# Layer 0's first block rearranged: x on two DMA queues, other loads issued later, tables loaded ahead, and PReLU's two signs computed on ScalarE

## The chip, the cores and the metric

The kernel runs on one core of a Trainium2 chip. The core has a matrix engine (TensorE, "PE" in the profile, with weight loads as "PEld"), a vector engine (VectorE, "DVE"), a scalar engine that computes activations from loaded tables (ScalarE, "ACT"), a general engine (GpSimd, "POOL") and SyncE ("SP"), which here only issues DMAs. Each engine takes its instructions in its own fixed order, and engines wait for each other through semaphores. ScalarE can issue DMAs too; these stand in its order between its computations.

The metric is device time in microseconds (us) of one execution. Before the change it is 2460.86 us, the median of 4 runs from 2460.74 to 2461.31.

## What is computed

The input is x of 4 images, 128 channels and 64 x 64 pixels, in float32. Layer 0 normalises x by groups of channels, makes two 64-channel projections and one of 128 channels by 1x1 convolutions with a PReLU each, and attends over all 4096 pixels. Layer 1 (a gated attention by running sums, and a routed feed-forward net) follows and is not touched.

```python
def _prelu(x, a):
    return jnp.where(x >= 0, x, a * x)
def _conv1x1(x, w, b, a):
    y = jnp.einsum('oc,nchw->nohw', w, x) + b[None, :, None, None]
    return _prelu(y, a)
...
e1 = _conv1x1(x, w1, b1, a1).reshape(N, -1, HW)
e2 = _conv1x1(x, w2, b2, a2).reshape(N, -1, HW)
asm = _conv1x1(x, wa, ba, aa).reshape(N, C, HW)
score = jax.nn.softmax(jnp.einsum('nci,ncj->nij', e1, e2), axis=2)
out = jnp.einsum('nij,ncj->nci', score, asm)
...
x = x + _L0_conv_ref(_gn(x), ...)          # layer 0
t = _to_tokens(x)
t = t + _L1_attn_ref(_ln_t(t), ...)        # layer 1
t = t + _L1_ffn_ref(_ln_t(t), ...)
```

PReLU can be written in several ways: max(y, 0) + a min(y, 0), which the kernel used, and relu(y) + (-a) relu(-y), which it uses after the change.

## The kernel before

**Tiling.** An image ("batch" b, 0 to 3) is 128 channels by 4096 pixels. It is cut into 8 blocks of 512 pixels (`NBLK`). A block k goes through these steps, each named by the tile that it makes:

- `stat(k)` (L371): VectorE's statistics of x over the block; `chain0` to `chain2` (L374 to L390) aggregate them, average them over channel groups with two small matmuls `pg`, and take a root on ScalarE, `std` (L389). That root is the only use of the sqrt table in this stretch; the exponentials use another table.
- `normal(k)` (L397): VectorE makes the normalised block `xn`.
- `project(k)`: TensorE multiplies by both projections' weights in two halves of the rows, `pe` (L416). ScalarE copies the first half out with the bias, `y` (L418); VectorE adds the second, also `y` (L419), here called the add; `prelu` makes `z` (L404) and `ee` (L407) on VectorE. Then four DMAs spread `ee` over the partitions: two copies for the queries, `e1` (L426), and two for the keys, `e2` (L429). This is the spread.
- `value(k)`: TensorE makes `pa` (L438), VectorE adds bias and second half in `ya` (L442, L445; the second is called yb in the text), then `prelu` makes `za` (L404) and `am` (L407).

`pe`, `pa` and the small matmuls share one PSUM buffer, so the projection of a block waits until yb of the block before has been computed, and `pa` waits for the add.

**Attention.** For each batch and each block `qb` of queries there are 16 steps p, each over two groups of 128 keys. `probs` multiplies keys and queries, `sc` (L471, two PSUM buffers), and ScalarE takes the exponential, `pr` (L475, three buffers); VectorE accumulates it, `acc` (L478, the first one a copy at L484). `weigh` multiplies values and `pr`, `av` (L496). On TensorE the scores of step p+1 come ahead of the weighing of step p. Step p needs keys and values of block p // 2. One step of scores and weighing takes TensorE 2.58 us. `finish` (L530 on), nine steps into the next query block, transposes the result and adds it to the residual `t`.

**Order.** All loops are unrolled, and a list scheduler fixes the order of each engine's instructions when the kernel is built. `tc.issue_after(i)` keeps what is written under it behind instruction i in that order. For batch 0, blocks 0 and 1 are prepared ahead of step 0, and blocks 2 to 7 at the even steps p = 0, 2, ..., 10 of the first query block (`own`, `work_off`). The blocks of batch b+1 are prepared during batch b, one piece (a projection or a value) at p = 2, 6 and 10.

**Loads.** The four loads of x of a batch (L327) and all loads of `t` (L521) and of layer 1's weights (`load_layer1`, L111 to L126) go through SP's queue, those of the small weights (L335) through ScalarE's. Before the change the scheduler put loads without a dependency early: loads of `t` and the layer-1 weights stand between x and the spreads of the first blocks. There are eight completion counters for DMAs, given out in turn over both queues; a DMA is issued only when the last one with its counter has landed.

The change touches `load_x`, `prelu`, `project`, `value`, and the places in the main loop that call `load_x`, `residual` and `load_layer1`.

Of the kernel before, what the change touches and what calls it, by code (L numbers as in the profile page):

```python
# [8 lines left out]
F32 = mybir.dt.float32  # L9
AF = mybir.ActivationFunctionType  # L10
# [8 lines left out]
def conv_attn_hybrid_kernel(  # L19
# [90 lines left out]
    def load_layer1(upper):  # L110
        nc.sync.dma_start(out=wks, in_=wkt.rearrange("d (h e) -> d h e", h=NH))  # L111
        nc.sync.dma_start(out=wvs, in_=wvt)

        qs = resid.tile([C, NH], F32, tag="qs", name="qs")
        nc.sync.dma_start(out=qs, in_=qt)
        nc.gpsimd.memset(qz, 0.0)
        for h in range(NH):
            nc.gpsimd.tensor_copy(qz[:, h, h // 4 : h // 4 + 1], qs[:, h : h + 1])

        for u in range(2):  # L120
            rows_u = slice(u * P // 2, (u + 1) * P // 2)
            nc.gpsimd.tensor_copy(mask[rows_u], upper[rows_u, rows_u])
        for z in range(2):
            nc.sync.dma_start(out=gws[:, z, :], in_=gwt)
            nc.sync.dma_start(out=gbs[z * E : (z + 1) * E, :], in_=gb)
        nc.sync.dma_start(out=fb1s, in_=fb1)  # L126
# [184 lines left out]
    with ExitStack() as l0:  # L311
# [8 lines left out]
        ps_av = pool("l0av", space=PSUM)  # L320
        qs_p = pool("l0q", NBLK + 1)

        def load_x(b):
            xs = one.tile([P, N], F32, tag="x", name=f"x_{b}")
            for q in range(4):
                cols = bass.ts(q, N // 4)
                nc.sync.dma_start(out=xs[:, cols], in_=x[b, :, cols])  # L327
            return xs

        xs_of = {0: load_x(0)}  # L330

        def load(name, shape, *parts):
            s = wp.tile(list(shape), F32, tag=name, name=name)
# [14 lines left out]
        aas = load("aas", [P, 1], (every[:1], aa.to_broadcast([P, 1])))  # L348
        bas = load("bas", [P, C], (every, ba.to_broadcast([P, C])))


        gavg = wp.tile([P, P], F32, tag="gavg", name="gavg")
        make_block_diagonal(nc, gavg, C // 32)
        nc.vector.tensor_scalar_mul(gavg, gavg, 32.0 / C)

        queries, keys_of, values_of = {}, {}, {}

        def preparation(b):

            xs = xs_of[b]  # L360
            stats = small.tile([P, NBLK, 6], F32, tag="stats", name=f"stats_{b}")
            mv = small.tile([P, 2], F32, tag="mv", name=f"mv_{b}")
            gst = small.tile([P, 4], F32, tag="gst", name=f"gst_{b}")
            std = small.tile([P, 2], F32, tag="std", name=f"std_{b}")

            e2 = big.tile([P, NCH // 2, P], F32, tag="e2", name=f"e2_{b}")
            am = big.tile([P, NCH, C], F32, tag="am", name=f"am_{b}")
            keys_of[b], values_of[b] = e2, am

            def stat(k):  # L370
                nc.vector.bn_stats(stats[:, k, :], xs[:, bass.ts(k, BLK)])  # L371

            def chain0():
                nc.vector.bn_aggr(mv, stats)  # L374

            def chain1():
                pg = ps_x.tile([P, 2, BLK], F32, tag="x", name=f"pg_{b}")
                nc.tensor.matmul(pg[:, 0, 0:1], gavg, mv[:, 0:1], start=True, stop=True)
                nc.vector.tensor_copy(gst[:, 0:1], pg[:, 0, 0:1])
                nc.vector.tensor_sub(gst[:, 1:2], mv[:, 0:1], gst[:, 0:1])  # L380
                nc.vector.scalar_tensor_tensor(
                    out=gst[:, 2:3], in0=gst[:, 1:2], scalar=gst[:, 1:2], in1=mv[:, 1:2],
                    op0=ALU.mult, op1=ALU.add,
                )

            def chain2():
                pg = ps_x.tile([P, 2, BLK], F32, tag="x", name=f"pg2_{b}")
                nc.tensor.matmul(pg[:, 0, 0:1], gavg, gst[:, 2:3], start=True, stop=True)
                i = nc.scalar.activation(std[:, 0:1], pg[:, 0, 0:1], AF.Sqrt, bias=eps5)  # L389
                nc.vector.reciprocal(std[:, 1:2], std[:, 0:1])  # L390
                return i.ins

            xn_of = {}

            def normal(k):
                xn = tmp.tile([P, BLK], F32, tag="xn", name=f"xn_{b}_{k}")
                nc.vector.tensor_scalar(  # L397
                    out=xn, in0=xs[:, bass.ts(k, BLK)], scalar1=gst[:, 0:1],
                    scalar2=std[:, 1:2], op0=ALU.subtract, op1=ALU.mult,
                )  # L400
                xn_of[k] = xn

            def prelu(dst, y, z, a):
                nc.vector.tensor_scalar(  # L404
                    out=z, in0=y, scalar1=0.0, scalar2=a, op0=ALU.min, op1=ALU.mult
                )
                nc.vector.scalar_tensor_tensor(  # L407
                    out=dst, in0=y, scalar=0.0, in1=z, op0=ALU.max, op1=ALU.add
                )

            def project(k):

                xn = xn_of[k]
                pe = ps_x.tile([P, 2, BLK], F32, tag="x", name=f"pe_{b}_{k}")
                for u, h in enumerate(halves):
                    nc.tensor.matmul(pe[:, u, :], w12[h, :], xn[h, :], start=True, stop=True)  # L416
                y = tmp.tile([P, BLK], F32, tag="y", name=f"y_{b}_{k}")
                nc.scalar.activation(y, pe[:, 0, :], AF.Identity, bias=b12)  # L418
                nc.vector.tensor_add(y, y, pe[:, 1, :])  # L419
                z = tmp.tile([P, BLK], F32, tag="z", name=f"z_{b}_{k}", bufs=1)  # L420
                ee = tmp.tile([P, BLK], F32, tag="ee", name=f"ee_{b}_{k}")
                prelu(ee, y, z, a12)
                e1 = qs_p.tile([P, BLK], F32, tag="e1", name=f"e1_{b}_{k}")
                queries[b, k] = e1
                for h in halves:
                    nc.sync.dma_start(out=e1[h, :], in_=ee[halves[0], :])  # L426
                by = ee.rearrange("r (j u p) -> r j u p", u=2, p=P)
                for u, h in enumerate(halves):
                    nc.sync.dma_start(  # L429
                        out=e2[h, bass.ts(k, CPB // 2), :], in_=by[halves[1], :, u, :]  # L430
                    )

            def value(k):
                xn = xn_of[k]
                pa = ps_x.tile([P, 2, CPB, C], F32, tag="x", name=f"pa_{b}_{k}")
                for c in range(CPB):
                    for u, h in enumerate(halves):
                        nc.tensor.matmul(  # L438
                            pa[:, u, c, :], xn[h, bass.ts(c, P)], was[h, :], start=True, stop=True
                        )  # L440
                y = tmp.tile([P, CPB, C], F32, tag="y", name=f"ya_{b}_{k}")
                nc.vector.tensor_tensor(  # L442
                    y, pa[:, 0], bas.unsqueeze(1).to_broadcast([P, CPB, C]), ALU.add
                )
                nc.vector.tensor_add(y, y, pa[:, 1])  # L445
                z = tmp.tile([P, CPB, C], F32, tag="z", name=f"za_{b}_{k}", bufs=1)
                prelu(am[:, bass.ts(k, CPB), :], y, z, aas)

            first = [lambda k=k: stat(k) for k in range(NBLK)] + [chain0]
            chain = [chain1, chain2]  # L450
            blocks = []
            for k in range(NBLK):
                blocks.append((lambda k=k: normal(k), lambda k=k: project(k)))
                blocks.append((lambda: None, lambda k=k: value(k)))
            return first, chain, blocks
# [62 lines left out]
        def residual(b, qb):  # L518

            at = b * NCH + qb * CPB  # L520
            nc.sync.dma_start(  # L521
                out=t[:, bass.ds(at, CPB), :],
                in_=xtok[bass.ds(at * P, CPB * P), :].rearrange("(c p) d -> p c d", p=P),
            )
# [33 lines left out]

        first, chain, blocks = preparation(0)
        for f in first + chain:  # L560
            f()
        own = blocks
        work_off(own, 4)
        nxt = probs(*steps[0])
# [2 lines left out]
        for n, (b, qb, p) in enumerate(steps):  # L567
            pr = nxt
            if own and p % 2 == 0:
                work_off(own, 2)  # L570
                if not own:
                    xs_of[1] = load_x(1)
            if n + 1 < len(steps):
                nxt = probs(*steps[n + 1])
            weigh(b, qb, p, pr)
# [4 lines left out]
            if b + 1 < B:  # L580
# [4 lines left out]
                    last_root = chain.pop(0)()  # L585
                if qb == q0 and p == 15:
                    blocks[0][0]()
            if p == 1:
                residual(b, qb)
            if p == 9 and done:  # L590
                finish(*done)
            if p in (11, 12) and done:
# [8 lines left out]
            if (b, qb, p) == (0, 1, 0):  # L601
                upper = wp.tile([P, P], F32, tag="upper", name="upper")
                make_upper_triangular(nc, upper)
                load_layer1(upper)
            if qb > q0 and p in (2, 6, 10) and b + 1 < B and blocks:
                blocks.pop(0)[1]()
                if blocks:
                    blocks[0][0]()
                elif b + 2 < B:
                    xs_of[b + 2] = load_x(b + 2)  # L610
            if p == NPR - 1:
                copied, fold = collect(b, qb)
                if n + 1 < len(steps):
# [691 lines left out]
```

## Time and profile before

| What | us |
|---|---|
| median of 4 runs | 2460.86 |
| the profiled execution: its time | 2460.14 |
| the profiled execution: its span | 2458.4 |
| TensorE busy (share of span) | 2376.6 (97%) |
| VectorE busy | 1520.0 (62%) |
| ScalarE busy | 1150.8 (47%) |
| TensorE's share of the chain that ended last | 94% |
| the exponentials, L475: 512 of 128x1024, mean | 1.024 |
| the accumulating adds, L478: 480 of 128x1024, mean | 1.222 |
| prelu on VectorE, L404: 64 of 128x512, mean | 0.486 |
| prelu on VectorE, L407: 64 of 128x512, mean | 0.693 |
| layer 1's first projection (L703) starts at | 1466.68 |

The span runs from the first to the last instruction that the profiler saw; the time has a little around it. "Busy" of TensorE is modelled: a busy TensorE is not one at its peak, but where it has no gap, no other engine holds it. A share of the whole span says little here, since the stages differ: layer 0's start, the long run of attention steps, and layer 1 have to be read one by one. The mean granted clock is 0.989.

### The profile page before, as it was taken

The page shows a single profiled execution, that of the slowest core. Times are in us where ns is not written, and L with a number is a line of the kernel's source. Part 1 is how long each engine was busy: PE and PEld are TensorE (multiplying, and loading weights), DVE is VectorE, ACT ScalarE, POOL GpSimd, SP SyncE. Part 2 cuts the span into 40 slices and gives each one's busy share as a digit, 9 for nine tenths or more (in the row PEclk, how much of TensorE's full clock was granted, in tenths as well). Part 3 has the DMA queues.
Part 4 walks back from the last instruction along what each step waited for, and adds up shares of the span by engine and source line. Part 5 has one row for each costly group of instructions (what it writes and reads, how often), then busy time and mean ns, then how long its engine had stood idle before and what let it go on. Part 6 is the DMA issues. An engine that isn't in the chain of part 4 may idle for free.

```text
span 2458.4 us, 46253 instructions
## 1 busy us (share of the span) xinstructions
PE 2376.6 (97%) x19732; PEld 1610.8 (66%) x19732; DVE 1520.0 (62%) x2680; ACT 1150.8 (47%) x1495; POOL 307.0 (12%) x370
## 2 busy tenths in 40 slices
PE   5999999999999999999999998999999999999797
PEld 3678777787777777776877764555555556555543
DVE  6766666666656666655555555666666766756524
ACT  2344343443343433434434335666666666665341
POOL 0000000000000000000000002333333333334000
PEclk9999999999999999999999999999999999999898
DMA  8100010000100000000000001212111111121495
GB/s 226 55 13 14 14 48 1 13 7 16 48 5 1 14 14 9 14 5 1 1 1 1 1 1 36 53 37 52 38 45 45 44 46 37 37 53 37 164 357 203
DMA packets 60583, 111.07 MB, mean 45 GB/s; under 512 B 10193, under 2 KB 35409, under 8 KB 60241
## 3 DMA queue, kind: packets, MB, share of 16 engines
q1 hardware_dynamic: 59072, 107.77, 14.9%
q8 instruction: 156, 2.56, 0.4%
q10 hardware_dynamic: 1296, 0.26, 0.1%
q14 instruction: 59, 0.48, 0.1%
HBM read 86.38 MB, written 8.91 MB: 39 GB/s over the span
## 4 chain that ended last, share of the span: by engine, by line
PE 94%; DVE 3%; ACT 1%; DMA 1%; issue 0%; SPq 0%; ACTq 0%; DVEq 0%
PE av L496 35%; PE sc L471 18%; PE pk L703 9%; PE pv L821 9%; PE po L857 4%; PE pt L837 2%; PE ps L722 2%; PE ph L1149 1%; PE otr L535 1%; PE po L864 1%; PE pa L438 1%; PE pl L912 1%; PE pe L416 1%; PE pp L988 1%; PE po L1176 1%; PE otr L1190 1%
## 5 line engine op out<-in xcount | busy, mean ns | idle before, releaser
L496 PE MATMUL av<-pr,am 64*128 64x512 f32 x4096 | 1092.3, 590 | 0.0
L475 ACT ACTIVATE pr<-sc 128x1024 f32<-128x1024 f32 x512 | 524.4, 1024 | 787.5 <-PE sc L471 718.7
L478 DVE TENSOR_TENSOR acc<-acc,pr 128x1024 f32<-128x1024 f32 x480 | 586.6, 1222 | 413.4 <-ACT pr L475 413.3
L496 PEld LDWEIGHTS av<-pr,am 64*128 64x128 f32 x4096 | 668.2, 187 | 233.5 <-issue 25.4
L471 PE MATMUL sc<-e,e 64*128 64x512 f32 x2048 | 652.0, 593 | 2.4 <-DMA e<-ee 2.4
L471 PEld LDWEIGHTS sc<-e,e 64*128 64x128 f32 x2048 | 336.8, 188 | 102.4 <-issue 16.7
L703 PE MATMUL pk<-xt,wks 128*128 128x512 f32 x512 | 244.2, 617 | 6.4 <-DVE inside L637 4.2
L821 PE MATMUL pv<-wvs,xt 128*128 128x512 f32 x512 | 226.8, 596 | 2.1 <-ACT v L825 2.1
L825 ACT ACTIVATE v<-pv 128x512 f32<-128x512 f32 x256 | 152.7, 597 | 69.7 <-PE pv L821 69.6
L705 ACT ACTIVATE ks<-pk 128x512 f32<-128x512 f32 x256 | 148.7, 597 | 63.0 <-PE pk L703 62.7
L821 PEld LDWEIGHTS pv<-wvs,xt 128*128 128x128 f32 x512 | 97.1, 191 | 121.1 <-issue 115.8
L809 DVE TENSOR_TENSOR em<-em,rb 128x1024 f32<-128x1024 f32 x64 | 79.5, 1244 | 156.6 <-DMA rb<-rd 149.7
L703 PEld LDWEIGHTS pk<-xt,wks 128*128 128x128 f32 x512 | 92.3, 193 | 114.3 <-issue 81.7
L857 PEld LDWEIGHTS po<-v,em 64*64 64x64 f32 x4096 | 111.4, 133 | 26.7 <-DVE before L847 26.7
L711 POOL MEMSET ew<- 128x1024 f32 x1 | 1.0, 952 | 1022.9 <-PE pa L438 1022.9
L800 POOL TENSOR_TENSOR em<-et,mask 128x1024 f32<-128x1024 f32 x64 | 120.4, 1902 | 9.2 <-ACT et L787 9.2
L96 POOL TENSOR_SCALAR xg<-t,gmv,grs 128x128 f32<-128x128 f32 x120 | 95.1, 805 | 194.9 <-DVE grs L92 139.6
L857 PE MATMUL po<-v,em 64*64 64x128 f32 x4096 | 119.2, 271 | 0.0
L759 DVE RECIPROCAL rr<-rr 128x512 f32<-128x512 f32 x32 | 107.3, 3353 | 1.1
L744 ACT ACT_TABLE_LOAD x24 | 30.8, 1283 | 119.0 <-DVE ss L743 119.0
L745 POOL COPY state<-mm 128x1 f32<-128x1 f32 x32 | 20.7, 646 | 509.2 <-DVE mm L739 509.0
L847 DVE TENSOR_TENSOR before<-before,pt 128x128 f32<-128x128 f32 x256 | 72.7, 284 | 9.7 <-PE pt L837 3.8
(160 smaller groups left out, 2122.5 us busy)
## 6 DMA issues: line engine op xcount, KB each, us to landing
rb<-rd SPq DMA_DIRECT2D x128, 256.0 KB
fw<-in_fw_dram SPq DMA_DIRECT2D x64, 512.0 KB
x<-in_x_dram SPq DMA_DIRECT2D x16, 512.0 KB
t<-in_xtok_dram SPq DMA_DIRECT2D x32, 256.0 KB
e<-ee SPq DMA_DIRECT2D x64, 128.0 KB
out_dram<-t SPq DMA_DIRECT2D x16, 512.0 KB
e<-ee SPq DMA_DIRECT2D x64, 64.0 KB
rd<-rr SPq DMA_DIRECT2D x64, 8.0 KB
```

The costliest lines, as they stand in the source:

```text
L96: i = engine.tensor_scalar(out=dst, in0=t[:, chunk, :], scalar1=mean, scalar2=rs, op0=ALU.subtract, op1=ALU.mult)
L471: nc.tensor.matmul(sc[:, u, :], e2[halves[u], p, :], e1[halves[u], :], start=True, stop=True)
L475: nc.scalar.activation(pr, sc, AF.Exp)
L478: added.append(nc.vector.tensor_add(acc, acc, pr).ins)
L496: nc.tensor.matmul(av, am[h, j, :], pr[h, u, :], start=(j == 0), stop=(j == NCH - 1))
L703: nc.tensor.matmul(pk, wks[:, h, :], xt, start=True, stop=True)
L705: nc.scalar.activation(ks, pk, AF.Silu)
L759: inverse = nc.vector.reciprocal(rr, rr).ins
L800: nc.gpsimd.tensor_tensor(em, eq.unsqueeze(2).to_broadcast([P, 2 * NH, H2]), mask.unsqueeze(1).to_broadcast([P, 2 * NH, H2]), ALU.mult,)
L821: nc.tensor.matmul(pv.rearrange("p h d -> p (h d)"), xt[:, bass.ts(2 * q + s, P)], wvs[:, bass.ts(m, BLK)], start=True, stop=True,)
L825: last = nc.scalar.activation(v[:, bass.ts(m, HPB), :], pv, AF.Silu).ins
L857: nc.tensor.matmul(po[s * H2 : (s + 1) * H2, u, q, :], aas[q][half, s, h, :], vs[2 * q + s][half, h, :], start=(q == 0 and h == 0), stop=F ...
```

## The change

The four quarters of batch 0's x go alternately through SP's and ScalarE's queue; later batches use SP's alone. The two negated slopes are computed once (`neg`). A first activation with a sqrt loads that table while x is loading, and one with an exponential, put behind the root, loads the other table. In `prelu`, z becomes relu(-y) and y becomes relu(y), both on ScalarE, except z of block 0 of batch 0, which VectorE makes; one VectorE operation joins them. `z` gets two buffers instead of one. The spread of block 0 of batch 0 goes half through each queue, and its four DMAs are issued half by half. Loads of batch 1's x, of `t` and of layer 1 are kept behind the latest spread, and `t` of a query block is loaded from step 5 on instead of step 1.

```diff
-        def load_x(b):
+        def load_x(b, queues):
             xs = one.tile([P, N], F32, tag="x", name=f"x_{b}")
             for q in range(4):
                 cols = bass.ts(q, N // 4)
-                nc.sync.dma_start(out=xs[:, cols], in_=x[b, :, cols])
+                queues[q % len(queues)].dma_start(out=xs[:, cols], in_=x[b, :, cols])
             return xs
-        xs_of = {0: load_x(0)}
+        xs_of = {0: load_x(0, (nc.sync, nc.scalar))}
...
+        neg = wp.tile([P, 2], F32, tag="neg", name="neg")
+        nc.vector.tensor_scalar_mul(neg[:, 0:1], a12, -1.0)
+        nc.vector.tensor_scalar_mul(neg[:, 1:2], aas, -1.0)
+        seed = wp.tile([P, 2], F32, tag="seed", name="seed")
+        nc.scalar.activation(seed[:, 0:1], eps5, AF.Sqrt)
...
-            def prelu(dst, y, z, a):
-                nc.vector.tensor_scalar(
-                    out=z, in0=y, scalar1=0.0, scalar2=a, op0=ALU.min, op1=ALU.mult
-                )
+            def prelu(dst, y, z, minus_a, negative):
+                if negative is nc.vector:
+                    nc.vector.tensor_scalar(
+                        out=z, in0=y, scalar1=-1.0, scalar2=0.0, op0=ALU.mult, op1=ALU.max
+                    )
+                else:
+                    nc.scalar.activation(z, y, AF.Relu, scale=-1.0)
+                nc.scalar.activation(y, y, AF.Relu)
                 nc.vector.scalar_tensor_tensor(
-                    out=dst, in0=y, scalar=0.0, in1=z, op0=ALU.max, op1=ALU.add
+                    out=dst, in0=z, scalar=minus_a, in1=y, op0=ALU.mult, op1=ALU.add
                 )
...
-                z = tmp.tile([P, BLK], F32, tag="z", name=f"z_{b}_{k}", bufs=1)
+                z = tmp.tile([P, BLK], F32, tag="z", name=f"z_{b}_{k}")
-                prelu(ee, y, z, a12)
+                prelu(ee, y, z, neg[:, 0:1], nc.vector if (b, k) == (0, 0) else nc.scalar)
-                for h in halves:
-                    nc.sync.dma_start(out=e1[h, :], in_=ee[halves[0], :])
+                queues = (nc.sync, nc.scalar) if (b, k) == (0, 0) else (nc.sync, nc.sync)
                 by = ee.rearrange("r (j u p) -> r j u p", u=2, p=P)
-                for u, h in enumerate(halves):
-                    nc.sync.dma_start(
+                for u, (h, queue) in enumerate(zip(halves, queues)):
+                    queue.dma_start(out=e1[h, :], in_=ee[halves[0], :])
+                    moved = queue.dma_start(
                         out=e2[h, bass.ts(k, CPB // 2), :], in_=by[halves[1], :, u, :]
                     )
+                if (b, k) != (0, 0):
+                    sent.append(moved.ins)
...
-                prelu(am[:, bass.ts(k, CPB), :], y, z, aas)
+                prelu(am[:, bass.ts(k, CPB), :], y, z, neg[:, 1:2], nc.scalar)
...
         for f in first + chain:
-            f()
+            root = f()
+        with tc.issue_after(root):
+            nc.scalar.activation(seed[:, 1:2], eps5, AF.Exp)
...
                 if not own:
-                    xs_of[1] = load_x(1)
+                    with tc.issue_after(sent[-1]):
+                        xs_of[1] = load_x(1, (nc.sync,))
...
-            if p == 1:
-                residual(b, qb)
+            if p == 5:
+                with tc.issue_after(sent[-1]):
+                    residual(b, qb)
...
-                load_layer1(upper)
+                with tc.issue_after(sent[-1]):
+                    load_layer1(upper)
```

More of the change, by code (lines that the diff above doesn't have):

```diff
@@ L354, in conv_attn_hybrid_kernel @@
         nc.vector.tensor_scalar_mul(gavg, gavg, 32.0 / C)
-        queries, keys_of, values_of = {}, {}, {}
+        queries, keys_of, values_of, sent = {}, {}, {}, []
         def preparation(b):
@@ L445, in value @@
                 nc.vector.tensor_add(y, y, pa[:, 1])
-                z = tmp.tile([P, CPB, C], F32, tag="z", name=f"za_{b}_{k}", bufs=1)
-                prelu(am[:, bass.ts(k, CPB), :], y, z, aas)
+                z = tmp.tile([P, CPB, C], F32, tag="z", name=f"za_{b}_{k}")
+                prelu(am[:, bass.ts(k, CPB), :], y, z, neg[:, 1:2], nc.scalar)
             first = [lambda k=k: stat(k) for k in range(NBLK)] + [chain0]
@@ L609, in conv_attn_hybrid_kernel @@
                 elif b + 2 < B:
-                    xs_of[b + 2] = load_x(b + 2)
+                    xs_of[b + 2] = load_x(b + 2, (nc.sync,))
             if p == NPR - 1:
```

## The prediction

> **What bounds the kernel now.** I read the whole-run table first (TensorE busy 97% of 2458.4 us, the chain that ended last 94% TensorE), then busy time by stretch, to see where TensorE is not full. Columns: stretch, its length, busy us and counts of TensorE, weight loads, VectorE, ScalarE, GpSimd, then granted clock, DMA share, GB/s.
>
> ```profile
> 0.00:10.00 10.00, 0.00 (x0) 0.00 (x0) 3.97 (x8) 0.00 (x0) 2.94 (x16) 1.00 0.64 185
> 10.00:20.00 10.00, 1.18 (x4) 1.00 (x4) 2.74 (x10) 1.54 (x2) 1.02 (x8) 1.00 0.78 251
> ...
> 34.00:52.00 18.00, 16.19 (x94) 7.61 (x92) 16.82 (x26) 5.48 (x6) 0.00 (x0) 1.00 1.09 270
> 52.00:60.00 8.00, 4.98 (x35) 2.77 (x33) 6.03 (x10) 1.71 (x2) 0.00 (x0) 1.00 1.19 247
> 60.00:84.00 24.00, 22.05 (x137) 11.93 (x136) 19.55 (x27) 8.48 (x10) 0.00 (x0) 1.00 0.49 142
> 84.00:1300.00 1216.00, 1216.00 (x6431) 919.03 (x6429) 769.21 (x1139) 496.12 (x507) 0.95 (x1) 1.00 0.05 12
> ```
>
> From 84 us on TensorE never waits in layer 0, so the edit can gain only in the first 84 us; later it can only lose. Next the timeline of the head (start, duration, engine, line, what; in brackets the idle time before and its releaser):
>
> ```profile
> 0.81 6.62 SPq L327 DMA_DIRECT2D x<-in_x_dram  x4
> ...
> 14.30 1.29 DVE L371 BATCH_NORM_STATS2 stats<-x 128x6 f32<-128x512 f32 x2 [4.12 <-DMA x<-in_x_dram]
> 15.62 0.37 DVE L374 BATCH_NORM_AGGREGATE mv<-stats 128x2 f32<-128x48 f32 x1
> ...
> 18.01 1.28 ACT L389 ACT_TABLE_LOAD   x1 [18.01 <-DMA qs<-in_qt_dram]
> 19.30 0.26 ACT L389 ACTIVATE std<-pg,eps 128x1 f32<-128x1 f32 x1
> ```
>
> The last quarter of x lands at 14.30, so the root ends at 19.56: nothing of block 0 can start before. SP's third and fourth issues of x, seen in narrow windows, are at 5.10 and 7.11, since in this program a DMA waits for the landing of the one that had its completion counter before it. Then the blocks, on the same timeline:
>
> ```profile
> 43.02 8.88 SPq L521 DMA_DIRECT2D t<-in_xtok_dram  x11
> ...
> 52.01 1.43 SPq L426 DMA_DIRECT2D e<-ee  x2
> ...
> 58.91 1.28 PE L471 MATMUL sc<-e,e 64*128 64x512 f32 x4 [2.37 <-DMA e<-ee]
> ...
> 61.56 1.21 PE L416 MATMUL pe<-xn,w 64*128 64x512 f32 x4
> ```
>
> Block 3's spread sits behind eleven loads of t, and TensorE waits 2.37 us for it. The projections of blocks 4 to 7 start at 51.12, 61.56, 69.55 and 77.38: 7.8 to 8.0 us apart but for that stall. In later batches (148 us) one projection looks so:
>
> ```profile
> 148.11 0.69 ACT L418 ACTIVATE y<-pe,b 128x512 f32<-128x512 f32 x1 [1.55 <-PE pe L416]
> ...
> 148.83 0.69 DVE L419 TENSOR_TENSOR y<-y,pe 128x512 f32<-128x512 f32 x1 [1.01 <-ACT y L418]
> 148.97 1.02 ACT L475 ACTIVATE pr<-sc 128x1024 f32<-128x1024 f32 x1 [0.17 <-PE sc L471]
> ...
> 151.20 2.03 PE L496 MATMUL av<-pr,am 64*128 64x512 f32 x8
> ```
>
> The exponential ends at 149.99 and is wanted at 151.20: 1.2 us to spare. No ReLU runs on ScalarE before; the nearest rows are other one-input passes over 128x512 from SBUF:
>
> ```profile
> 2408.24 0.63 ACT L1170 ACTIVATE hs<-hs 128x512 f32<-128x512 f32 x1 [1.54 <-DVE hs L1165]
> 2408.78 0.71 ACT L1206 ACTIVATE lg<-lg,rden 128x512 f32<-128x512 f32 x1
> ```
>
> One takes 0.63, and an independent successor starts 0.54 after it. From below, copies of this size take 0.58 to 0.59 (L508, L695).
>
> **The head: x, loads, tables.** All four quarters are issued by about 1.7 us, two per queue, and t and the layer-1 weights (some 1.5 MB issued by 17 us) no longer follow them. Lower bound of the landing: 2.1 MB at the 397 GB/s of 72 to 75 us, when batch 1's x moved almost alone, takes 5.3 us: 7.3. Upper: batch 1's four loads, issued from 68.06, moved until about 77, 8.9 us: 9.8. I take 9.0: the first 8 us of before moved 1.69 MB (sum of its 1-us stretches), and the missing 0.4 MB takes 1.0. Each queue's second quarter now ends at about the same moment, so four statistics stay behind the landing, two pairs of 1.29, then the scaling of gavg (0.21) and the aggregate (0.37): 12.2 against 15.99, a gain of 3.8 (3.0 to 5.5). The sqrt table (1.28) is loaded ahead: the last small load on ScalarE's queue waits for x's last quarter, so its issues end near 9.9 (0.34 + 0.56 later), table and seed near 11.5, and the root is wanted at 12.2 + 1.9 = 14.1. Gain 1.28; were the issues 2.6 us later, nothing. The two negated slopes are tiny VectorE operations (0.16 each) in the gap where VectorE waits for the group averages (0.68); their loads need to have landed by 12; block 0's spread, issued by 27.74, was used at 29.88, and at 2.1 us they make it. The exp table goes behind the root, where ScalarE is idle 2.99 us (L418); 1.28 + 0.26 fits. Without that gap it would cost 1.5. Head: **-5.1** (-6.8 to -4.3).
>
> [...]
>
> **Blocks 0 to 7.** In the built program each queue keeps its own order. Per block VectorE loses two operations of 0.49 (L404), ScalarE gains four ReLUs. TensorE's order is the same but for one matmul. The exp table load at 30.86 (1.28) is gone, but z of block 1 now stands ahead of exp 0, which also waits for VectorE's add (0.72 + 0.54): nothing gained. The two-queue spread of block 0 (1.2 instead of 2.45) lands before projection 1 is through on TensorE, which is next in its order: nothing. Up to projection 4, VectorE being the full engine (16.82 of 18), I get 0.5 us gained (0 to 1.5).
>
> From block 3 on a ring forms. With z and r the two ReLUs of the projection, za and ra those of the value, ScalarE runs za, ra, exp(even), y, z, exp(odd), r; VectorE runs acc(even), add, acc(odd), ee, ya, xn, yb, am. Start to start, by rows of 45 to 60 us: za 0.66, ra 0.54, exp 1.05, acc 1.14, add 0.72, z 0.54, exp 1.05, acc 1.13, ee 0.61, ya 0.60, xn 0.45, yb 0.71, and yb releases the next za: **9.2 us a block**, against 7.83 where TensorE and VectorE set the pace. From projection 4 to 7 that is 27.6 against 26.3 with the old stall inside: +1.3, so the removed t stall (2.4) is paid back with interest. After projection 7 the value's matmuls wait for an add that is behind acc (3.6 after the projection, 2.5 before): +1.1; and exp 12 stands behind za and ra of block 7, so the weighing of step 12 waits: +0.9. Sum: -0.5 + 1.3 + 1.1 + 0.9 = **+2.8**. Bounds: ReLUs of 0.59 take off 0.8, and a better start 0.5 more: +1.5; without the 0.09 overlaps, a dozen times 0.09 and a slower start: +4.5.
>
> [...]
>
> **Moved loads.** Batch 1's x (wanted by the statistics after 122 us), the layer-1 weights (after 1460) and each t (wanted 20 steps of 2.58 later) land long before; SP is idle there. If one were late the finish behind it would wait, at 2 us a load.
>
> **Batches 1 to 3.** 24 projections: y ends 148.80, add 149.52, z starts 149.55, exp 150.09 to 151.11, wanted at 151.20. It fits with 0.06 to 0.11 left. I take +0.3 (0 to 2.9, which is 0.12 each). The value's ReLUs fall between two exponentials with 0.16 or more left. The spread there starts 2 us later and has tens of us.
>
> **Sum.** -5.1 + 2.8 + 0.3 = -2.0. The profiled execution took 2460.14 around its span of 2458.4, the median is 2460.86; the same difference gives **2458.9**. Own range: -6.8 + 1.5 to -4.3 + 4.5 + 2.9, so 2455.6 to 2464.0.
>
> **Rivals.**
> - *The ring does not bind.* If the exponentials are not held, blocks keep 7.83: 3 x 1.37 less, -6.1, 2454.8. For it: VectorE sheds 0.97 a block and was full. Against: the order is fixed and each link above is a true wait.
> - *Slower: the exponential of the later batches is late.* From 0.1 us of extra delay on, every projection stalls TensorE, where nothing hides it. If add is held by an acc, a third of its 1.22, 0.4 each, is 24 x 0.4 = 9.6: +7.6, 2468.5. For it: the margin falls from 1.2 us to 0.1. Against: at 148 us VectorE has been idle 1.01 before that add.
> - *x lands no earlier.* Only the table is won: -1.28 + 2.8 + 0.3 = +1.8, 2462.7. For it: the DMA share is 0.7 to 1.0 from 10 to 15 us. Against: much of that is t and weights, now gone.
>
> **Chances.** Forecast 0.65, ring free 0.15, late exponentials 0.12, x no earlier 0.08. A measurement of this kernel can tell 0.2%, 4.9 us, from no change. Faster: 0.15 and 0.02 from the forecast's edge, 0.17. Slower: 0.12 and 0.01, 0.13. Same: 0.70. The range goes from below the free ring, 2454.3, up to 2465.0, leaving out most of the late exponentials.
>
> **What would show it.** Last statistics ending near 11.6 and the root near 14.4 (head); projections 4 to 7 about 9.2 apart, with ScalarE's y idle before it only through its queue (ring); in 150 to 1300 us TensorE still full (margin). Projections 8 us apart, or TensorE idle ahead of L510 once per projection, would prove the forecast wrong.

## The result and the profile after

| | median us | runs | lowest to highest |
|---|---|---|---|
| before | 2460.05 | 60 | 2457.54 to 2461.97 |
| after | 2455.80 | 40 | 2454.22 to 2458.77 |

The ratio is 0.9983, with a 95% interval from 0.9979 to 0.9988: 4.2 us less, 0.17%. The profiled execution of the changed kernel took 2457.41 around a span of 2455.7, so it is one of its longer ones: the two profiles differ by 2.7 us, the medians by 4.2. All differences below that are read from a trace are differences of single executions; layer 1 alone, from its first projection to the end, took between 989.6 and 992.0 us in those of this case.

The timeline of the changed kernel's head (start, duration, engine, line, what; in brackets the idle time before and its releaser):

```profile
0.81 0.90 ACTq L327 DMA_DIRECT2D x<-in_x_dram  x2
0.81 0.86 SPq L327 DMA_DIRECT2D x<-in_x_dram  x2
...
5.72 5.01 DVE L378 BATCH_NORM_STATS2 stats<-x 128x6 f32<-128x512 f32 x8 [4.65 <-DMA x<-in_x_dram]
...
10.26 1.28 ACT L356 ACT_TABLE_LOAD   x1 [10.26 <-DMA a<-in_a_dram]
...
10.77 0.37 DVE L381 BATCH_NORM_AGGREGATE mv<-stats 128x2 f32<-128x48 f32 x1
...
13.10 0.26 ACT L396 ACTIVATE std<-pg,eps 128x1 f32<-128x1 f32 x1 [1.34 <-PE pg L395]
13.38 1.28 ACT L577 ACT_TABLE_LOAD   x1
...
16.35 0.69 ACT L429 ACTIVATE y<-pe,b 128x512 f32<-128x512 f32 x1 [1.48 <-PE pe L427]
```

All four quarters of x are issued by 1.71. VectorE starts its eight statistics at 5.72 and runs through them; a narrow window shows one stop of 0.06 us, before the fifth at 8.25. The first table load ends at 11.54, ahead of the root at 13.10; the second, at 13.38, ends before `y` needs ScalarE at 16.35. The root ends at 13.36 instead of 19.56. Busy time by stretch shows why the statistics run through (stretch, length, busy us and counts of TensorE, weight loads, VectorE, ScalarE, GpSimd, then clock, DMA share, GB/s):

```profile
4.00:5.00 1.00, 0.00 (x0) 0.00 (x0) 0.00 (x0) 0.00 (x0) 0.00 (x0) 1.00 1.04 418
...
7.00:8.00 1.00, 0.00 (x0) 0.00 (x0) 1.00 (x3) 0.00 (x0) 0.00 (x0) 1.00 1.02 343
8.00:9.00 1.00, 0.00 (x0) 0.00 (x0) 0.94 (x3) 0.00 (x0) 0.00 (x0) 1.00 0.30 51
```

The DMA share is 0.92 to 1.04 from 3 to 8 us, then 0.30 and 0.01 in the next two: x has landed by about 8.1. VectorE's first four statistics take it to 8.19, so a still earlier landing of the last quarters would gain only the 0.06. Now one turn of the blocks, on the timeline:

```profile
44.35 0.63 ACT L416 ACTIVATE za<-ya 128x512 f32<-128x512 f32 x1 [3.09 <-DVE ya L459]
...
45.55 1.01 ACT L489 ACTIVATE pr<-sc 128x1024 f32<-128x1024 f32 x1
...
46.59 1.22 DVE L492 TENSOR_TENSOR acc<-acc,pr 128x1024 f32<-128x1024 f32 x1 [0.16 <-ACT pr L489]
47.73 0.68 DVE L430 TENSOR_TENSOR y<-y,pe 128x512 f32<-128x512 f32 x1
48.45 0.63 ACT L416 ACTIVATE z<-y 128x512 f32<-128x512 f32 x1 [1.31 <-DVE y L430]
48.47 2.02 PE L452 MATMUL pa<-was,xn 64*128 64x128 f32 x16 [2.01 <-DVE y L430]
48.98 1.01 ACT L489 ACTIVATE pr<-sc 128x1024 f32<-128x1024 f32 x1
...
52.88 0.68 DVE L459 TENSOR_TENSOR ya<-ya,pa 128x512 f32<-128x512 f32 x1
53.60 0.63 ACT L416 ACTIVATE za<-ya 128x512 f32<-128x512 f32 x1 [3.09 <-DVE ya L459]
```

From za to the next za, 44.35 to 53.60, each line starts when the one that it waits for has ended, on ScalarE or VectorE in turn. TensorE has no part in it and waits 2.01 us for the add. The turn takes 9.25 us. And a projection of a later batch, on the same timeline:

```profile
146.75 0.63 ACT L416 ACTIVATE z<-y 128x512 f32<-128x512 f32 x1 [0.75 <-DVE y L430]
147.29 1.01 ACT L489 ACTIVATE pr<-sc 128x1024 f32<-128x1024 f32 x1
147.54 1.17 PE L485 MATMUL sc<-e,e 64*128 64x512 f32 x4
...
148.40 2.03 PE L510 MATMUL av<-pr,am 64*128 64x512 f32 x8
```

The exponential ends at 148.30 and is used at 148.40: the margin of 1.2 us has shrunk to 0.1, and TensorE isn't held.

Where the time went, from the two traces: the root ends 6.2 earlier (19.56 to 13.36); from the root to the scores of step 16, the first of the second query block, it takes 76.8 instead of 73.4; from there to layer 1's first projection 1373.65 instead of 1373.75.

### The profile page after: what moved, and what is told of

Its sections match the earlier page's. It is cut to its first block, busy times and chain, and to the rows that moved or that the text cites. A ratio compares the mean times of both kernels' runs of the same rounds, so it can differ in the third digit from the quotient of the medians.

```text
span 2455.7 us, 46279 instructions
## 1 busy us (share of the span) xinstructions
PE 2376.1 (97%) x19732; PEld 1582.6 (64%) x19732; DVE 1490.6 (61%) x2619; ACT 1218.7 (50%) x1624; POOL 309.2 (13%) x370
## 4 chain that ended last, share of the span: by engine, by line
PE 90%; DVE 5%; ACT 3%; DMA 1%; issue 1%; SPq 0%; DVEq 0%; ACTq 0%
PE av L510 35%; PE sc L485 18%; PE pk L722 9%; PE pv L840 8%; PE po L876 4%; PE pt L856 2%; PE ps L741 2%; PE ph L1168 1%; PE otr L549 1%; PE po L883 1%; PE pp L1007 1%; PE pe L427 1%; PE pa L452 1%; PE pl L931 1%; PE po L1195 1%
## 5 line engine op out<-in xcount | busy, mean ns | idle before, releaser
L510 PE MATMUL av<-pr,am 64*128 64x512 f32 x4096 | 1050.5, 591 | 0.7 <-ACT pr L489 0.7
L510 PEld LDWEIGHTS av<-pr,am 64*128 64x128 f32 x4096 | 636.1, 187 | 253.7 <-issue 45.3
L485 PE MATMUL sc<-e,e 64*128 64x512 f32 x2048 | 607.5, 592 | 0.0
L485 PEld LDWEIGHTS sc<-e,e 64*128 64x128 f32 x2048 | 315.0, 187 | 103.3 <-issue 22.0
```

What stands on the lines that cost most here:

```text
L485: nc.tensor.matmul(sc[:, u, :], e2[halves[u], p, :], e1[halves[u], :], start=True, stop=True)
L510: nc.tensor.matmul(av, am[h, j, :], pr[h, u, :], start=(j == 0), stop=(j == NCH - 1))
```

## The experiments

Each kernel ran beside the kernel before on the same chip, and its ratio is against those runs. "Root" is the end of `std` in its trace; "blocks" is the time from there to the scores of step 16. The kernels ran at three times, on three chips; where two of them are compared below by their medians, the ratios give up to 1.2 us less, and the intervals are 2 to 3.5 us to each side, so root and blocks of the traces say where such a difference lies.

| kernel | median us | ratio, 95% interval | root | blocks |
|---|---|---|---|---|
| before | 2460.05 | | 19.56 | 73.4 |
| after | 2455.80 | 0.9983, 0.9979 to 0.9988 | 13.36 | 76.8 |
| after, once more | 2455.63 | 0.9983, 0.9974 to 0.9992 | 13.40 | 76.8 |
| PReLU on VectorE | 2449.15 | 0.9953, 0.9939 to 0.9966 | 13.28 | 70.0 |
| ReLUs only in batches 1 to 3 | 2450.06 | 0.9958, 0.9945 to 0.9972 | 13.38 | 70.2 |
| one ReLU for two | 2450.02 | 0.9959, 0.9945 to 0.9972 | 13.37 | 70.6 |
| ReLUs alone | 2464.89 | 1.0016, 1.0007 to 1.0025 | 20.87 | 78.6 |
| x on one queue | 2459.68 | 0.9994, 0.9985 to 1.0003 | 16.27 | 76.8 |
| PReLU on VectorE, x on one queue | 2452.51 | 0.9964, 0.9951 to 0.9978 | 16.51 | 70.1 |
| no early tables | 2458.94 | 0.9994, 0.9985 to 1.0003 | 14.72 | 78.6 |
| loads free | 2459.59 | 0.9996, 0.9987 to 1.0005 | 14.98 | 78.7 |
| PReLU on VectorE, loads free | 2457.26 | 0.9985, 0.9976 to 0.9994 | 13.84 | 78.8 |
| z twice as wide | 2465.56 | 1.0020, 1.0011 to 1.0029 | 13.54 | 77.1 |

### Is it the ReLUs on ScalarE that form the ring?

PReLU on VectorE: the changed kernel with `prelu` as it was.

```diff
-        neg = wp.tile([P, 2], F32, tag="neg", name="neg")
...
-                    nc.scalar.activation(z, y, AF.Relu, scale=-1.0)
-                nc.scalar.activation(y, y, AF.Relu)
...
+                nc.vector.tensor_scalar(
+                    out=z, in0=y, scalar1=0.0, scalar2=a, op0=ALU.min, op1=ALU.mult
+                )
                 nc.vector.scalar_tensor_tensor(
-                    out=dst, in0=z, scalar=minus_a, in1=y, op0=ALU.mult, op1=ALU.add
+                    out=dst, in0=y, scalar=0.0, in1=z, op0=ALU.max, op1=ALU.add
                 )
```

> The changed kernel, with PReLU back on VectorE in all blocks (min and multiply, then max and add), all else kept. Ring theory: without ReLUs on ScalarE projections 4 to 7 are 7.8 us apart instead of the 9.3 of the changed kernel's trace (27.96 from projection 4 to 7, so 4.5 us less), and the value after projection 7 and step 12 wait 2 us less: some 6 us below the changed kernel, about 2449.5, 10 below before. Rival (VectorE's relief is what pays): VectorE gets 0.97 us a block back and was the full engine, so 4 to 6 us above the changed kernel, back at before or above.

It has the lowest median of this case, 2449.15, and comes out as the ring theory said. On its timeline, the projection, the add's followers and the next projection:

```profile
52.09 1.02 PE L419 MATMUL pe<-xn,w 64*128 64x512 f32 x4
...
54.60 0.49 DVE L407 TENSOR_SCALAR z<-y,a 128x512 f32<-128x512 f32 x1
54.62 1.16 PE L444 MATMUL pa<-was,xn 64*128 64x128 f32 x16 [0.65 <-DVE y L422]
...
59.91 1.02 PE L419 MATMUL pe<-xn,w 64*128 64x512 f32 x4
```

Projections start 7.82 apart and TensorE waits 0.65 a block instead of 2.01. The root is where the changed kernel has it; the blocks take 6.8 less. So VectorE, which the change relieves, has time for its two extra passes a block.

ReLUs alone: the kernel before with the new `prelu`, `neg` and two buffers for z, and nothing else of the change.

```diff
+        neg = wp.tile([P, 2], F32, tag="neg", name="neg")
...
+                    nc.scalar.activation(z, y, AF.Relu, scale=-1.0)
+                nc.scalar.activation(y, y, AF.Relu)
```

> The kernel before with nothing changed but the PReLUs: negated slopes, both ReLUs on ScalarE, two buffers for z; loads, tables and queues as before. Ring theory: from the first root to the first scores of the second query block 76.8 us instead of 73.4, projections 9.2 apart from the fourth on; the stall behind the loads of t (2.4) stays and may add to it or be absorbed by it: +3.4 to +5.8 over the kernel before, 2464 to 2466. Rival (VectorE, the full engine of these blocks, is relieved and the ring is only a part of the other edits): 2 to 4 us faster than before, 2456 to 2458.

The median is 3.6 above the kernel before, at the lower end of what the ring theory gave, and the rival falls. The profiled execution (2465.69) is longer than the median: its blocks take 5.2 more than before, with 1.34 of the wait for the third block's spread left, and in it the last quarter of x came at 15.61 instead of 14.30, though it was issued no later; the edit doesn't explain this.

One ReLU for two: PReLU as y + (1 - a) relu(-y), so the second ReLU falls away and `neg` holds 1 - a.

```diff
-        nc.vector.tensor_scalar_mul(neg[:, 0:1], a12, -1.0)
-        nc.vector.tensor_scalar_mul(neg[:, 1:2], aas, -1.0)
+        for c, a in enumerate((a12, aas)):
+            nc.vector.tensor_scalar(
+                out=neg[:, c : c + 1], in0=a, scalar1=-1.0, scalar2=1.0, op0=ALU.mult, op1=ALU.add
+            )
...
-                nc.scalar.activation(y, y, AF.Relu)
```

> The changed kernel with one ReLU instead of two in each PReLU, (1 - a) relu(-y) + y, so ScalarE gains two passes a block and not four. Ring theory: without r and ra the same links make za 0.54 + exp 1.05 + acc 1.14 + add 0.72 + z to the end of acc(odd) 2.72 + ya 0.60 + xn 0.45 + yb 0.71 = 7.9 us a block instead of 9.2, so within 1 us of the kernel with the PReLU on VectorE (2449 to 2451), projections 7.8 to 8.0 apart, and no drop of the granted clock in the first 85 us. Rival (it is the place of any ReLU between the exponentials that costs, not the number): 2454 to 2456, as the changed kernel, projections about 9 apart.

2450.02, with projections 4 to 7 at 44.46, 52.44, 60.41 and 68.39: 7.98 apart, where the links gave 7.9. A ReLU on ScalarE costs next to nothing as such; the sum of the links decides, and two passes fewer bring it down to within 0.16 of the 7.82 without ReLUs.

### Do the ReLUs cost anything in the later batches?

ReLUs only in batches 1 to 3: the changed kernel, with this at the head of `prelu`.

```diff
+                if b == 0:
+                    nc.vector.tensor_scalar(
+                        out=z, in0=y, scalar1=0.0, scalar2=a12 if minus_a is neg12 else aas,
+                        op0=ALU.min, op1=ALU.mult,
+                    )
+                    nc.vector.scalar_tensor_tensor(
+                        out=dst, in0=y, scalar=0.0, in1=z, op0=ALU.max, op1=ALU.add
+                    )
+                    return
```

> The changed kernel with batch 0's PReLUs on VectorE (as in the kernel before the change) and both ReLUs on ScalarE only in batches 1 to 3. Theory (the ReLUs cost in the ring of the first eight blocks alone, and the 0.10 us left for the exponential in the later batches is enough): within 1 us of the kernel with every PReLU on VectorE, 10 to 12 us faster than the kernel before, TensorE without a wait from 95 to 1450. Rival (part of the 6.6 us between the changed kernel and that one lies in the 24 later projections): 2 us or more slower than it.

2450.06, 0.9958 against 0.9953 for the kernel with every PReLU on VectorE: no difference that these intervals can tell. From step 16 to layer 1 both traces take 1373.4 us. All of the ReLUs' cost lies in the first eight blocks.

z twice as wide: how near the 24 later projections are to the edge. `wide` is given in batches 1 to 3 only.

```diff
-                    nc.scalar.activation(z, y, AF.Relu, scale=-1.0)
+                    if wide is not None:
+                        nc.scalar.activation(
+                            wide, y.unsqueeze(1).to_broadcast([P, 2, BLK]), AF.Relu, scale=-1.0
+                        )
+                    else:
+                        nc.scalar.activation(z, y, AF.Relu, scale=-1.0)
```

> The changed kernel in which, in batches 1 to 3, the first ReLU of a projection runs over its input twice in one instruction (1024 columns instead of 512, the second half is not used); the order of the instructions is the same on every engine, and the two buffers for z become one for the projections and one for the values. From the exponential's 1.02 I take 1.06 for it instead of 0.63, so the exponential behind it ends 0.43 later. Margin theory (0.10 us is left): TensorE waits about 0.33 ahead of the weighing, 24 times: +8 over the changed kernel (+6 to +10), 3 to 5 us slower than the kernel before. Rival (the exponential has more room than the trace says, or TensorE catches up in its queue): +0 to +1.5.

It is 9.9 us slower than the changed kernel beside it (2465.56 against 2455.63). Its timeline at the same projection:

```profile
147.30 1.06 ACT L417 ACTIVATE z<-y 128x1024 f32<-128x1024 f32 x1 [0.75 <-DVE y L435]
148.08 1.17 PE L491 MATMUL sc<-e,e 64*128 64x512 f32 x4
148.26 1.01 ACT L495 ACTIVATE pr<-sc 128x1024 f32<-128x1024 f32 x1
...
149.32 1.99 PE L516 MATMUL av<-pr,am 64*128 64x512 f32 x8
```

The weighing starts 1.24 after the scores, where the changed kernel has 0.86 (147.54 to 148.40): 0.38 late for 0.43 more on ScalarE, so only 0.05 of the apparent 0.10 was room. From step 16 to layer 1 its trace is 8.8 longer, 0.37 for each of 24 projections. Look at what is missing in these lines: no bracket stands before the weighing, and the waits of TensorE from 95 to 1445 us are an empty list in this kernel too. The modelled end of the scores (1.17) covers the gap. From start to start one sees it.

### What the parts of the head are worth

x on one queue: the changed kernel with x through SP's queue.

```diff
-        xs_of = {0: load_x(0, (nc.sync, nc.scalar))}
+        xs_of = {0: load_x(0, (nc.sync,))}
```

> The changed kernel, with batch 0's x through SP's queue alone. The built program then lets the third and fourth quarter wait for landings again, as before, but t and layer-1 weights stay behind the spreads. If the two queues brought the early landing: the last statistics move back by 2 us or more and the time rises by as much. If the loads taken out of the way brought it: the fourth quarter, issued near 7.1, lands near 9.3 and only its own two statistics stay behind it, so the chain starts within 1 us of the changed kernel and the time rises by 0 to 1 us.

It went the first of the two ways: it is 3.9 slower than the changed kernel by the medians, 2.7 by the ratios, and the root is 2.9 later. But the timeline shows one thing that the edit moved unasked:

```profile
8.89 0.15 DVE L352 TENSOR_SCALAR neg<-a 128x1 f32<-128x1 f32 x1 [1.86 <-DMA a<-in_a_dram]
...
10.97 0.15 DVE L353 TENSOR_SCALAR neg<-aas 128x1 f32<-128x1 f32 x1 [1.33 <-DMA aas<-in_aa_dram]
```

The scheduler has put the two negations among the statistics here, and VectorE waits there for the slopes. To keep that apart, the same edit was made to the kernel with PReLU on VectorE, which has no `neg`.

> The changed kernel with the PReLU on VectorE (2449.2) and batch 0's x on SP's queue alone; there are no negated slopes that could stand among the statistics. Counter theory: the third and fourth issues of x wait as before (about 5 and 7 us), the last quarter lands near 10.8, the root is 1.0 to 1.6 us later than 13.3: 2450.2 to 2451. Rival one (the two queues are worth all that the one-queue kernel lost): +3 to +4, 2452 to 2453. Rival two (only the order of the other loads matters): no difference.

It is 3.4 above that kernel (by the ratios, 0.9964 against 0.9953, 2.7), and the root is 3.2 later, so nearly all of it is the queue itself, as the first rival said; the counter theory had expected a root at most 1.6 later. Its timeline:

```profile
5.01 2.26 SPq L327 DMA_DIRECT2D x<-in_x_dram  x2
...
8.99 1.29 DVE L374 BATCH_NORM_STATS2 stats<-x 128x6 f32<-128x512 f32 x2 [1.27 <-DMA x<-in_x_dram]
...
12.59 1.29 DVE L374 BATCH_NORM_STATS2 stats<-x 128x6 f32<-128x512 f32 x2 [2.18 <-DMA x<-in_x_dram]
```

The third and fourth issues fall between 5.01 and 7.27, since each waits for the landing of an earlier load with its counter, and x is complete for VectorE only at 12.59. In between the DMA engines run low, as its stretch from 8 to 9 us shows; then the last quarter moves nearly alone, and from 11 to 12 it finishes:

```profile
8.00:9.00 1.00, 0.00 (x0) 0.00 (x0) 0.01 (x1) 0.94 (x2) 0.00 (x0) 1.00 0.33 41
9.00:10.00 1.00, 0.00 (x0) 0.00 (x0) 1.00 (x2) 0.00 (x0) 0.00 (x0) 1.00 0.59 211
10.00:11.00 1.00, 0.00 (x0) 0.00 (x0) 0.41 (x2) 0.00 (x0) 0.00 (x0) 1.00 0.86 239
11.00:12.00 1.00, 0.00 (x0) 0.00 (x0) 0.00 (x0) 0.00 (x0) 0.00 (x0) 1.00 0.31 114
```

From 8 to 9 us 41 GB/s move, because the fourth issue is not out in time to follow the third, and the last quarter gets 211 and 239, where two queues moved 343 to 418 from 3 to 8 us. Whether four issues on one queue that need not wait for counters would do as well as two queues, no run shows.

No early tables: the changed kernel without the two seeds.

```diff
-        nc.scalar.activation(seed[:, 0:1], eps5, AF.Sqrt)
...
-            nc.scalar.activation(seed[:, 1:2], eps5, AF.Exp)
```

> The changed kernel without the two early table loads. By the sum of the prediction: the sqrt table comes back on the way to the root, +1.28 us, and the exp table stands between z of block 1 and the first exponential; there it delays step 0 by 1.28, of which the ring that forms later may take up all or none: +1.3 to +2.6 us over the changed kernel. Rival (both loads were hidden or are taken up later by the ring): 0 to +0.5.

3.1 slower by the medians, 2.7 by the ratios, a little more than expected. The root is 1.36 later, one table load (1.28) and its start. The blocks take 1.9 more, all of it before projection 4, so the ring doesn't hide the second table. But a table load is 1.28: in this kernel the scheduler also put the first accumulation, `acc`, behind a `ya`, `xn`, yb and `ee` instead of ahead of them, so not all of the 1.9 is the table's.

Loads free: the changed kernel with the loads of `t`, of batch 1's x and of layer 1 no longer kept behind a spread; then the same edit to the kernel with PReLU on VectorE.

```diff
-                    with tc.issue_after(sent[-1]):
-                        xs_of[1] = load_x(1, (nc.sync,))
+                    xs_of[1] = load_x(1, (nc.sync,))
...
-            if p == 5:
-                with tc.issue_after(sent[-1]):
-                    residual(b, qb)
+            if p == 1:
+                residual(b, qb)
...
-                with tc.issue_after(sent[-1]):
-                    load_layer1(upper)
+                load_layer1(upper)
```

> The changed kernel, with the loads of t, of batch 1's x and of layer 1 free again to stand between x and the spreads as before. x still has its two queues. Theory: x shares the DMA engines with 1.5 MB and lands 1 to 3 us later, and one spread is stuck behind loads of t; the ring, slower than TensorE, takes up a part of that stall: +2 to +4 us over the changed kernel. Rival (the two queues alone hold x's lead and the ring hides the stall): within 0.5 us of the changed kernel.

3.8 slower (3.2 by the ratios), the size that was expected, but not in the expected way. VectorE's statistics end at 10.83, so x isn't delayed; the small loads are. The first table starts at 11.98 instead of 10.26 and is still in time. What holds the root, 1.6 later, is a negation that waits for its slope and stands on VectorE ahead of the group averages:

```profile
13.37 0.15 DVE L352 TENSOR_SCALAR neg<-a 128x1 f32<-128x1 f32 x1 [2.14 <-DMA a<-in_a_dram]
```

The blocks take 1.9 more.

> The changed kernel with the PReLU on VectorE (2449.2) and the loads of t, batch 1's x and layer 1 free to be issued at once, as in the kernel before. Theory: the small loads and so the tables come later (root +1.6, as in the changed kernel with free loads), and with no ring to hide it the third block's spread stands behind the loads of t again (2.4 us of TensorE idle): +3.5 to +5.5, 2452.7 to 2454.7. Rival (the spread's wait is absorbed later in the blocks): the head's 1.6 alone, 2450.8.

8.1 slower than with the loads held back, and more than either theory said. Its runs spread from 2452.3 to 2460.6, and the profiled one is 2.5 above the median. Without `neg` its root is only 0.6 later, but the blocks take 8.8 more. On the timeline:

```profile
15.21 4.68 SPq L527 DMA_DIRECT2D t<-in_xtok_dram  x7
...
20.91 0.79 SPq L433 DMA_DIRECT2D e<-ee  x1
...
27.22 2.15 PE L477 MATMUL sc<-e,e 64*128 64x512 f32 x4 [2.80 <-DMA e<-ee]
```

The very first scores wait 2.80 for block 0's spread, issued by 21.70 but right behind seven loads of `t`: the DMA share is 1.19 from 20 to 30 us. In the kernel before, `t`'s last load ahead of that spread was issued by 19.85 and the spread only from 25.24 on; its DMA share is 0.00 from 23 to 25 us, and its first scores don't wait. TensorE waits again, 2.33 at 56.80, as the kernel before does once (2.37), and here the granted clock falls behind that wait (last section): scores and weighing take 4.34 to the next projection instead of 2.58. In the changed kernel with its loads free only the first of these waits shows, with 0.94. So in this pair holding the loads back is worth more in the kernel without the ring, 8.1 against 3.8.

### The changed kernel once more

> The changed kernel once more, on this chip and beside these two. It should come 3 to 6 us faster than the kernel before; its profile should show projections 4 to 7 about 27 to 29 us apart in all, and one stretch of a few us with a granted clock below 1.00 in the first 85 us, perhaps at another place than the first time. If the clock stays at 1.00 there, the drop is not the kernel's.

2455.63, and projections 4 to 7 start at 44.55, 55.49, 63.32 and 72.56, 28.0 in all. The drop of the clock came back at nearly the same place, 49.58 instead of 48.58 (last section).

## Why the prediction was right, and where its sizes were off

The forecast was 2458.9 with its own range from 2455.6 to 2464.0, and no change beyond 0.2% as the likeliest; the median is 2455.8 and the change 0.17%, near the edge that was named.

**Head, -5.1 forecast, -6.2 measured.** This is the mis-sized term. The landing of x was taken as 9.0, from the bytes that the kernel before moved in its first 8 us. That rate had the holes in it that come from late issues (236 GB/s from 3 to 4 us, 254 from 7 to 8); without them the engines moved 369 to 418 GB/s from 3 to 7 us, and x was there by 8.1. The chain behind was right: four statistics after the landing (2.5, forecast 2.6). The fifth statistic starts at 8.25, 0.75 before the 9.0, and from there to the end of the aggregate, at 11.14 and not 12.2, it takes 2.89 where the forecast added 3.16: the last statistic, gavg's scaling and the aggregate overlap a little on VectorE. Both tables are hidden as said; without the early loads the kernel loses 3.1.

The second queue is worth about 3 us (the 3.2 of the root without `neg`), and what it saves is late issue: all four loads of x are issued by 1.71 with two queues, and the last two between 5.01 and 7.27 with one. So the rival "x lands no earlier" fell by the landing at 8.1.

**Blocks, +2.8 forecast, +3.4 measured.** Up to projection 4: -0.4 (forecast -0.5). From projection 4 to 7: 27.96 against 26.26, +1.7 (+1.3); three turns of 9.24 are 27.72, and the other 0.24 come with a drop of the clock (last section). From projection 7 to its value's matmuls: 3.63, +1.1 (+1.1). From there to the scores of step 16: 14.02 against 13.01, +1.0 (+0.9), of which 0.74 is this wait, at step 12:

```profile
83.16 1.99 PE L510 MATMUL av<-pr,am 64*128 64x512 f32 x8 [0.74 <-ACT pr L489]
```

The 9.2 us of the ring are shown: where the clock stays up, turns take 9.24, and without the ReLUs 7.82, without half of them 7.98. The median is nearer to the 2454.8 of the rival "the ring does not bind" than to the forecast, but not for that rival's reason, since the ring does bind; it comes near by luck, through the head's extra 1.1 and the spread of the executions.

In the first eight blocks PReLU on VectorE is better by 6.8 us, for the ring's sake; in batches 1 to 3 the place makes no difference (1373.4 us from step 16 to layer 1 with either).

**Batches 1 to 3, +0.3 forecast, 0.0 measured.** The margin held in all 24 projections. The rival of the late exponentials fell, but it was 0.05 us away: 0.43 more on ScalarE cost 9.9 us, the size that the rival named.

**Sum.** -6.2 + 3.4 - 0.1 and +0.2 in layer 1 make the -2.7 by which the profiled executions differ; the other 1.5 of the medians' 4.2 lies between one execution and another. The second trace of the changed kernel, 2.5 shorter, has the same root and blocks; its layer 1 is 2.3 shorter.

What the prediction didn't ask is whether the parts help each other. Without the ReLUs the change is worth 11 us (PReLU on VectorE), and the ReLUs give back about 7 of them.

## What to carry to other kernels

Before work is moved from a full engine to an idle one, write down the loop that the two engines' fixed orders form and add its links: the idle engine's busy share says nothing (ScalarE was busy 4.81 of the 10 us from 60 to 70 while the ring bound), and the full engine may be better left full. In this kernel a sum near TensorE's own pace was nearly free (turns of 7.98 against 7.82), and what went beyond it was paid every turn (9.24). And where DMAs wait for completion counters, look at the times at which they are issued, not at the bytes alone: in this kernel the first loads were worth a second queue (the 3.2 of the root), and loads that nobody waited for yet belonged behind the ones that somebody did (3.8 and 8.1 us).

## What the runs showed of the hardware that was not expected

In the first 85 us the granted clock of TensorE falls to half, once and for 3.41 us, in eight of the thirteen traces. In the traces of the kernel before and of the changed one the recorded clock changes only at whole multiples of 3.41 us from the record's first entry (34.20 and 24.69 us; the changed kernel's drop begins after seven of them and ends after eight), so the time ahead of a drop can be cut into stretches of that length. The changed kernel, the stretch ahead of its drop, the drop, and the one behind:

```profile
45.17:48.58 3.41, 1.40 (x8) 0.36 (x6) 2.58 (x3) 2.10 (x4) 0.00 (x0) 1.00 0.26 56
48.58:51.99 3.41, 3.41 (x22) 2.40 (x24) 1.97 (x3) 1.93 (x3) 0.00 (x0) 0.50 0.01 2
51.99:55.40 3.41, 3.41 (x18) 1.55 (x16) 2.05 (x4) 1.77 (x3) 0.00 (x0) 1.00 0.53 114
```

The matmuls of `pa` at 48.47 take 2.02 instead of 1.16, and the weighing behind them 2.75 instead of 1.89. Half the clock for 3.41 us is 1.7 us of clock.

The drop is in the trace of every kernel whose TensorE waits about 2 us in turn after turn (the changed one twice, ReLUs alone, x on one queue, no early tables, loads free, wide z), and with PReLU on VectorE and loads free behind the wait of 2.33, between 48 and 81 us. It is in none of those whose projections are 7.8 to 8.0 apart (PReLU on VectorE with two queues and with one, one ReLU for two, ReLUs only in batches 1 to 3). The kernel before waits 2.37 once and has none. Which wait a drop follows can be read from the stretches: the one ahead of it has TensorE busy for 1.40 us in seven traces and 1.08 in the eighth, and no other stretch from the record's first entry to 95 us in any trace has less than 1.48 (wide z, at 54.40, with no drop behind it). The 2.37 of the kernel before is divided between two stretches, with 1.87 and 2.59 busy. So in these traces the drop goes with how the waits fall into the stretches, and not only with how long they are. No run was made to test this, and it gives no fixed limit: in layer 1, with matmuls of other shapes, drops also stand behind stretches with up to 2.03 busy (at 1460.97 us in the kernel before, at 1458.28 in the changed one).

In the changed kernel the drop costs little: the projections before and after it are 10.9 and 7.8 apart, 18.7 against 18.5 for two turns of 9.24, because the ring of ScalarE and VectorE sets the pace and TensorE has 2 us a turn to lose.

The joining operation took 0.75 with a slope from a tile as its scalar, where the one before (L407) took 0.69 with a constant; VectorE's gain per PReLU is 0.43, not 0.49. Block 0's `z`, on VectorE with two constants, took 0.43 where L404 with a slope took 0.49, the same 0.06. The arithmetic differs in both pairs too, so that the tile is the cause is not shown.
